# Splitting dt's weights ahead of the barrier, and projecting each last chunk behind the next chunk's moments

## The chip, the cores and the metric

One core of one Trainium2 chip runs the whole program in one launch. The metric is the device time in microseconds (us), median of the runs. All tensors are float32 in HBM; some are cut into three bfloat16 parts on the chip for TensorE.

## The reference, cut to what matters

Layer 0 is a linear attention over eight images of 128 x 128 x 128. Layer 1, the part that the change touches, is a selective scan:

```
xb  = silu(conv3x3(x @ Win[:, :256]) + conv_b)                     # the front
xs  = xb in 4 directions: rows, rows reversed, columns, columns reversed
dt, Bs, Cs = x_dbl[:8], x_dbl[8], x_dbl[9]      with x_dbl = xs @ Wxproj
delta = softplus(dt_weight @ dt + dt_bias)                         # the scan's first matmul
h_l = exp(delta * A) * h_(l-1) + delta * u * B_l ;   y_l = C_l * h_l + D * u
yz  = (sum of y over the directions) * silu(z)                     # "gate"
out = layernorm(yz) @ Wout                                         # "moments", then "project", "store"
```

The layer norm is over 256 channels, so it needs the mean of `yz` and of its square for each token before the result can be scaled; the product with `Wout` can be made before that and scaled afterwards.

## The kernel before, in words

The program has three stages: `layer0`, `layer1_front` and `layer1_scan`. In the last two, `in_order` fixes each engine's instructions, DMA issues included, in the order in which the Python code calls them. An engine or DMA queue that waits therefore holds up everything behind it. What decides about the time is the order inside `step` and which semaphore each instruction waits for.

**The front's end.** `layer1_front` walks eight images of 16 chunks. After an image, `leave(b)` writes its activation `ures` to HBM a second time with rows and columns exchanged: 32 copies into tiles named `turned` (line 635), done by ScalarE where `k % 5` is 1 or 3 and by VectorE otherwise, each followed by a 512 KB write on the SP queue (line 636). After copies 9 and 19, `split` cuts the rows of `dt`, `B` and `C` into three bfloat16 parts (lines 44, 46) and writes them (line 625). For the last image nothing else is left to be done, so the stage ends when the last `turned` write has landed.

**The scan's start.** A barrier over all engines (line 723) separates the stages. Behind it the SP queue loads the small tensors and `dt_weight` and `dt_bias` (line 737); VectorE splits both with `split3`, which is a cast, a subtraction, a cast, a subtraction and a cast; the six parts are written to HBM (lines 742, 744), and `weights` loads them back into the tiles `dtw` with ten small loads per direction (lines 825, 826). GpSimd clears these tiles first (line 760). Then SP issues `load_rows` (lines 865, 866) and `load` (line 872), which the first `delta` (line 883) and the first `weigh` (line 894) wait for.

**The scan's end.** N = 512 is the number of scan steps. When an image's last direction is done, its 16 chunks "leave" one per step: `leaving[n]` names the chunk of step n. For seven images that lies under the next image's scan. The last image's chunks leave in steps N to N+15 with nothing else to be done. I call these steps S0 to S15, and S16 the one after. In one of these steps the engines get, in this order:

- VectorE: `gate(now, 1)` (line 972: y times z, second half), `store` of the chunk before (line 1023, eight instructions into tile `r`), `variance(now)` (line 1005)
- ScalarE: `square(now, 1)` (line 975), `keep` (line 991, tile `sr`), `square_mean` (line 1001, `mv`), `square(next, 0)`
- TensorE: `moments(now)` (line 985, `pm`), `to_tokens(now)` (line 997, `pq`), `project(now)` (line 1017, `px`)
- GpSimd: `deviation` of the chunk before (lines 1009, 1010), `gate(next, 0)`, and in seven of the steps the DMA issue of `add_d` (line 856), which adds 1024 KB of `gs` to `y` in memory
- SP queue: two loads of `z` for the chunk after next (`fetch`, line 968), two stores to `out` (line 1027)

`pm` and `pq` share the one PSUM buffer with the tag `pt`, so the moments of a chunk also wait until `variance` of the chunk before has read `pq`. `z` has six buffers, two for each chunk, so `fetch` waits for the projection of the chunk three before it. `r` has two buffers, so a `store` waits until the store of the chunk before has landed.

Of the kernel before, what the change touches and what calls it, by code (L numbers as in the profile page):

```python
# [8 lines left out]
F32 = mybir.dt.float32  # L9
BF16 = mybir.dt.bfloat16  # L10
# [4 lines left out]
DRAM = bass.MemoryType.DRAM  # L15

P = 128
# [4 lines left out]
NC2 = 2  # L22
R = 8
K = 4
# [6 lines left out]
CH = 1024  # L31
# [9 lines left out]
def split3(nc, parts, x):  # L41

    for j in range(3):
        nc.vector.tensor_copy(parts[j], x)
        if j < 2:
            nc.vector.tensor_tensor(x, x, parts[j], ALU.subtract)
# [335 lines left out]


@with_exitstack
def layer1_front(ctx: ExitStack, tc, x1, win, conv_w, conv_b, wxp, d_par, ubs, xds, xps, gts, gs):

# [8 lines left out]
    nc = tc.nc  # L397
    const = ctx.enter_context(tc.tile_pool(name="l1c", bufs=1))
    big = ctx.enter_context(tc.tile_pool(name="l1b", bufs=1))
    wp = ctx.enter_context(tc.tile_pool(name="l1w", bufs=3))  # L400
# [34 lines left out]
    for j, d in enumerate(ON_PE):  # L435
        for c in range(NC2):
            dg = wp.tile([P, P], F32, name="dg1", tag="tb", bufs=4)
            nc.vector.tensor_scalar(dg, ident, cw[:, c, tap(*d) : tap(*d) + 1], None, ALU.mult)
            p = pm.tile([P, P], F32, name="pw", tag="m")
# [18 lines left out]
    N = B * NCH  # L458

    SEQ = (4, 6, 5, 7, 0, 1, 2, 3)  # L460
# [145 lines left out]
    def load_rows(b, i):  # L606
        r = slice(i * half, i * half + half)
        xws[b, i] = x = wp.tile([P, half, H], F32, name="xw", tag="d", bufs=2)
        nc.sync.dma_start(x, xds[b].rearrange("r (w h) -> w r h", h=H)[:, r, :])

    def split(b, i):

        r = slice(i * half, i * half + half)
        x = xws.pop((b, i))
        pt = pj.tile([P, half, P], F32, name="ptx", tag="pj")
        for j in range(half):
            nc.tensor.transpose(pt[:, j, :], x[:, j, :], ident)
        y = wp.tile([P, half, W], F32, name="xh", tag="tb", bufs=4)
        nc.scalar.copy(y, pt)
        for order, v in ((TURN, y), (NAT, x)):  # L620
            q = wp.tile([P, 3, half, P], BF16, name="parts", tag="tb", bufs=4)
            split3(nc, [q[:, j] for j in range(3)], v)
            dst = xps[b, order].rearrange("j r (a e) -> a j r e", e=P)
            for j in range(3):
                nc.sync.dma_start(dst[:, j, r, :], q[:, j])

    def leave(b):

        for i in range(2):
            load_rows(b, i)  # L630
        for k in range(NC2 * NCH):
            c, i = divmod(k, NCH)
            t = wp.tile([P, CW, W], F32, name="turned", tag="tc" if k % 3 == 2 else "tb", bufs=2 if k % 3 == 2 else 4)
            copy = nc.scalar.copy if k % 5 in (1, 3) else nc.vector.tensor_copy
            copy(t, uturn[:, c, i * CW : i * CW + CW, :])
            nc.sync.dma_start(ubs[b, TURN][c][:, i * CH : i * CH + CH], t.rearrange("p h w -> p (h w)"))
            if k % 10 == 9 and k < 20:
                split(b, k // 10)

    def step(n):  # L640

# [53 lines left out]


@with_exitstack
def layer1_scan(ctx: ExitStack, tc, ubs, xps, zs, gs, dtw, dtb, a_log, gamma, beta, w_out, out):

# [12 lines left out]
    nc = tc.nc  # L714
    const = ctx.enter_context(tc.tile_pool(name="l2c", bufs=1))
    big = ctx.enter_context(tc.tile_pool(name="l2b", bufs=1))
    wp = ctx.enter_context(tc.tile_pool(name="l2w", bufs=3))
    sm = ctx.enter_context(tc.tile_pool(name="l2s", bufs=4))
    px = ctx.enter_context(tc.tile_pool(name="l2px", bufs=3, space=PSUM))
    pe = ctx.enter_context(tc.tile_pool(name="l2pe", bufs=1, space=PSUM))  # L720
    dram = ctx.enter_context(tc.tile_pool(name="l2d", bufs=1, space=DRAM))

    tc.strict_bb_all_engine_barrier()

# [3 lines left out]
    nc.scalar.activation(sa, sa, AF.Exp)  # L728
    nc.vector.tensor_scalar(sa, sa, -1.0, None, ALU.mult)


    D2 = 2 * P
    wparts = dram.tile([3, R, K, D2], BF16, name="wparts")
    bparts = dram.tile([3, K, D2], BF16, name="bparts")
    for dst, src, rows in ((wparts, dtw.rearrange("k r d -> r k d"), R), (bparts, dtb.rearrange("o (k d) -> o k d", d=D2), 1)):
        x = wp.tile([rows, K, D2], F32, name="w32", tag="sp", bufs=2)
        nc.sync.dma_start(x, src)
        q = wp.tile([rows, 3, K, D2], BF16, name="w16", tag="ub", bufs=4)
        split3(nc, [q[:, j] for j in range(3)], x)
        for j in range(3):  # L740
            if rows == 1:
                nc.sync.dma_start(dst[j : j + 1], q[:, j])
            else:
                nc.sync.dma_start(dst[j], q[:, j])

# [10 lines left out]
    for i in range(3):  # L758
        t = const.tile([P, D2], BF16, name=f"dtw{i}")
        nc.gpsimd.memset(t, 0.0)  # L760
# [90 lines left out]
    ubt, sp, da = {}, {}, {}  # L851
# [122 lines left out]
    def square(m, hf):  # L974
        nc.scalar.activation(piece(m, hf), zt[m, hf], AF.Square)  # L975
# [56 lines left out]
    leaving, summed, fetched, weighed = {}, {}, {}, {}  # L1032
    for o in range(B):
        n = (o + 1) * K * NCH
# [11 lines left out]
    N = len(units)  # L1046

    def step(n):
        live = 0 <= n < N
        then = n + 1 < N  # L1050
        before = 1 <= n <= N
        now, last, soon, later = (leaving.get(n + i) for i in (0, -1, 1, 2))
        first = before and units[n - 1][0].place == 0
        if before:
            half1 = units[n - 1][0].first
            emit(n - 1, half1)
            if not first:
                gather(n - 1)
        if now and last:
            gate(*now, 1, nc.vector)  # L1060
        if before:
            emit(n - 1, 1 - half1)
        if n + 2 < N:
            load_rows(n + 2)
        if n in fetched:
            fetch(*fetched[n])
        if live:
            decay(n, 0)
        if now:
            square(now[1], 1)  # L1070
        if live:
            decay(n, 1)
            weigh(n, 0)
        if last:
            deviation(last[1])
        if live:
            weigh(n, 1)
        if now:
            moments(now[1])
        if live:  # L1080
            scan(n, 0)
            da.pop((n, 0))
        if last:
            for hf in range(2):
                store(*last, hf)
        if then:
            for c in range(NC2):
                delta(n + 1, c)
        if now:
            keep(now[1])  # L1090
        if then:
            soften(n + 1, 0)
        if now:
            to_tokens(now[1])
            square_mean(now[1])
        if then:
            soften(n + 1, 1)
        if live:
            scan(n, 1)
        if first:  # L1100
            ubt.pop(n - 1)
            if n + 3 < N:
                load(n + 3)
        if now:
            variance(now[1])
        if live:
            half1 = units[n][0].first
            spread(n, half1, "pc")
            spread(n, 1 - half1, "pt")
        if soon and now:  # L1110
            gate(*soon, 0, nc.gpsimd)
        elif soon:
            gate(*soon, 1, nc.gpsimd)
        elif later:
            gate(*later, 0, nc.gpsimd)
        if soon:
            square(soon[1], 0)
        if now:
            p = da.pop((n, 1)) if live else px.tile([P, CH], F32, name="px")
            for hf in range(2):  # L1120
                project(now[1], hf, p[:, hf * 512 : hf * 512 + 512])
        elif live and units[n][0].place == 0:
            da.pop((n, 1))
        if before and not first:
            add(n - 1)
            ubt.pop(n - 1)
        if n + 3 < N and not first:
            load(n + 3)
        if n in weighed:
            units[weighed[n]][0].weights()  # L1130
        if n in summed:
            add_d(*summed[n])
# [16 lines left out]
@with_exitstack  # L1149
def tile_kernel(ctx: ExitStack, tc, a, out):  # L1150
    dram = ctx.enter_context(tc.tile_pool(name="dram", bufs=1, space=DRAM))
    x1 = dram.tile([B, P, L], F32, name="x1")
    ubs = dram.tile([B, 2, NC2, P, L], F32, name="ubs")
    xds = dram.tile([B, R + 2, L], F32, name="xds")
    xps = dram.tile([B, 2, 3, R + 2, L], BF16, name="xps")
    zs = dram.tile([B, NC2, P, L], F32, name="zs")
    gts = dram.tile([2, NC2, P, NCH, NCH, CW * CW], F32, name="gts")
    gs = dram.tile([2, NC2, P, L], F32, name="gs")
    layer0(
        tc, a["x"], a["L0_conv_w_qkv"], a["L0_conv_w_out"], a["L0_conv_b_out"],  # L1160
        a["L0_conv_gamma"], a["L0_conv_beta"], a["L1_conv_Win"], x1, zs,
    )
    layer1_front(
        tc, x1, a["L1_conv_Win"], a["L1_conv_conv_w"], a["L1_conv_conv_b"], a["L1_conv_Wxproj"],
        a["L1_conv_D_param"], ubs, xds, xps, gts, gs,
    )
    layer1_scan(
        tc, ubs, xps, zs, gs, a["L1_conv_dt_weight"], a["L1_conv_dt_bias"], a["L1_conv_A_log"],
        a["L1_conv_gamma"], a["L1_conv_beta"], a["L1_conv_Wout"], out,
    )  # L1170

# [39 lines left out]
```

## Time and profile before

| what | value |
|---|---|
| median of 3 runs (lowest to highest) | 9557.71 us (9557.14 to 9560.87) |
| profiled execution: its own time / its span | 9559.43 us / 9557.7 us |
| busy: VectorE, GpSimd, ScalarE, TensorE | 85%, 75%, 75%, 66% |
| last `turned` write issued / first issue behind the barrier | 4835.1 us / 4840.8 us |
| first `rows` load of the scan issued | 4860.5 us |
| first and last `variance` of the last image (line 1005) | 9425.0 us / 9548.4 us |

Positions are microseconds from the start of the span. In timelines, a row is start, duration, engine, line, operation, output and inputs with shapes, and in brackets how long the engine had been idle and what ended that. Equal rows that follow closely are merged, with their count behind an x; such a row runs from the first start to the last end.

### The profile page before, as it was taken

How to read it: one execution, taken by the hardware profiler on the slowest of the kernel's cores; microseconds unless marked ns; L12 is line 12 of the kernel's file. 1: busy time of each engine (PE TensorE's matmuls, PEld its weight loads, DVE VectorE, ACT ScalarE, POOL GpSimd, SP SyncE). 2: the span in 40 equal slices, each digit the busy share in tenths (PEclk: the TensorE clock that was granted, in tenths of full speed). 3: DMA queues.
4: the chain of work that ended last, by engine and by line, in shares of the span. 5: the costliest groups of instructions: out<-in, count | busy, mean ns of one | idle time of the engine just before them, and what ended most of it. 6: DMA issues, size and time to landing. Idle time of an engine off the chain costs nothing. (4 is left out here: it accounts for less than half of the span.)

```text
span 9557.7 us, 89859 instructions
## 1 busy us (share of the span) xinstructions
PE 6331.1 (66%) x24352; PEld 3113.6 (33%) x24352; DVE 8131.2 (85%) x8188; ACT 7168.0 (75%) x8256; POOL 7193.5 (75%) x4361
## 2 busy tenths in 40 slices
PE   8999999988977788777923543636345363553736
PEld 5555655554322233222300321404123040220403
DVE  6667765563988898888979999999999999999996
ACT  5556655566977788777878888888888888888885
POOL 3445544454665488776849999999999999999997
PEclk9999999999988899888955665757557585665757
DMA  2332233313476678888765957759587695866858
GB/s 91 132 135 78 97 133 132 132 69 140 169 261 238 220 259 254 265 265 274 236 208 167 254 180 205 241 172 270 156 226 217 187 260 165 242 192 198 248 165 214
DMA packets 1034807, 1851.21 MB, mean 194 GB/s; under 512 B 274852, under 2 KB 500772, under 8 KB 1026112
## 3 DMA queue, kind: packets, MB, share of 16 engines
q1 hardware_dynamic: 999488, 1711.23, 54.1%
q0 software_dynamic: 34816, 134.23, 7.4%
q8 instruction: 199, 3.26, 0.1%
q14 instruction: 304, 2.49, 0.1%
HBM read 1153.03 MB, written 692.12 MB: 193 GB/s over the span
## 5 line engine op out<-in xcount | busy, mean ns | idle before, releaser
L894 POOL TENSOR_TENSOR ubt<-ubt,sp 128x1024 f32<-128x1024 f32 x1024 | 2458.0, 2458 | 157.9 <-ACT sp L887 90.7
L883 PE MATMUL px<-rows,dtw 128*128 128x512 bf16 x2048 | 952.9, 565 | 2234.3 <-DVE y L944 1062.6
L516 POOL TENSOR_TENSOR tap<-tap 128x1024 f32<-128x1024 f32 x512 | 1206.6, 2368 | 640.1 <-ACT tap L514 518.1
L524 DVE SCALAR_TENSOR_TENSOR acc<-xb,cw,acc 128x1024 f32<-128x1024 f32 x1024 | 1320.3, 1289 | 52.7 <-ACT tap L514 0.9
L887 ACT ACTIVATE sp<-px 128x1024 f32<-128x1024 f32 x1024 | 1046.0, 1024 | 419.0 <-PE px L883 344.3
L952 POOL TENSOR_TENSOR y<-y,ubt 128x512 f32<-128x512 f32 x768 | 1156.7, 1552 | 145.6 <-DVE ubt L925 145.3
L506 PE MATMUL acc<-xi,wt 128*128 128x512 f32 x2048 | 952.7, 608 | 385.8 <-ACT ures L531 385.4
L904 DVE TENSOR_TENSOR_SCAN ubt<-px,ubt 128x1024 f32<-128x1024 f32 x512 | 1176.5, 2330 | 25.4 <-POOL ubt L894 19.6
L902 DVE TENSOR_TENSOR_SCAN ubt<-px,ubt 128x1024 f32<-128x1024 f32 x512 | 1178.0, 2331 | 12.3 <-POOL ubt L894 6.1
L883 PEld LDWEIGHTS <-dtw 128*128 128x128 bf16 x2048 | 164.4, 109 | 3062.1 <-issue 868.4
L891 ACT ACTIVATE px<-sp,sa 128x1024 f32<-128x1024 f32 x1024 | 1110.2, 1109 | 6.1
L514 ACT ACTIVATE tap<-xb,cw 128x1024 f32<-128x1024 f32 x768 | 834.0, 1139 | 68.4 <-POOL tap L516 68.1
L887 ACT ACT_TABLE_LOAD x512 | 656.9, 1283 | 166.7 <-PE px L883 164.6
L282 POOL TENSOR_TENSOR q<-q,qs 128x512 f32<-128x512 f32 x256 | 272.0, 1063 | 638.5 <-DVE qs L281 638.5
L506 PEld LDWEIGHTS acc<-xi,wt 128*128 128x128 f32 x2048 | 383.8, 192 | 930.3 <-ACT ures L531 487.9
L891 ACT ACT_TABLE_LOAD x512 | 656.9, 1283 | 9.2
L1017 PEld LDWEIGHTS px<-wg,z 128*128 128x128 f32 x4096 | 560.5, 220 | 118.8 <-issue 113.7
L910 PE MATMUL pc<-rows,csel 128*128 128x512 bf16 x1024 | 515.5, 584 | 82.5 <-DVE rstd L1005 78.6
L1017 PE MATMUL px<-wg,z 128*128 128x128 f32 x4096 | 560.8, 303 | 0.0
L479 PE MATMUL pxb<-xi,wi 128*128 128x512 f32 x1024 | 495.8, 606 | 4.3 <-ACT xb L488 4.3
L944 DVE TENSOR_TENSOR y<-y,px 128x1024 f32<-128x1024 f32 x384 | 468.5, 1220 | 14.7 <-DVE px L932 0.5
L298 ACT ACTIVATE sq<-o 128x512 f32<-128x512 f32 x256 | 161.2, 630 | 423.0 <-DVE o L296 421.8
(155 smaller groups left out, 15151.2 us busy)
## 6 DMA issues: line engine op xcount, KB each, us to landing
ubt<-ubs SPq DMA_DIRECT2D x512, 1024.0 KB
zs<-z SPq DMA_DIRECT2D x512, 256.0 KB
ubs<-ures SPq DMA_DIRECT2D x256, 512.0 KB
ubs<-turned SPq DMA_DIRECT2D x256, 512.0 KB
z<-zs SPq DMA_DIRECT2D x256, 512.0 KB
y<-gs POOLq DMA_DIRECT2D x128, 1024.0 KB, 10.3
rows<-xps SPq DMA_DIRECT2D x1536, 60.0 KB
xi<-x SPq DMA_DIRECT2D x120, 576.0 KB
```

Of the source, the lines that this page charges most:

```text
L506: nc.tensor.matmul(acc[:, s, :], wt[:, j, c, :], x, start=(j == 0), stop=(j == len(ON_PE) - 1))
L514: nc.scalar.activation(t, at(n, c, *d), AF.Copy, scale=cw[:, c, tap(*d) : tap(*d) + 1])
L516: nc.gpsimd.tensor_tensor(sums[n, c], sums[n, c], t, ALU.add)
L524: nc.vector.scalar_tensor_tensor(acc, at(n, c, *d), cw[:, c, tap(*d) : tap(*d) + 1], acc, ALU.mult, ALU.add)
L883: nc.tensor.matmul(p[:, hf * 512 : hf * 512 + 512], sl.dw[:, c * P : c * P + P], src, start=True, stop=True)
L887: nc.scalar.activation(t, da[n, c], AF.Softplus)
L891: nc.scalar.activation(da[n, c], sp[n, c], AF.Exp, scale=sa[:, sl.s, c : c + 1])
L894: nc.gpsimd.tensor_tensor(ubt[n][:, c, :], ubt[n][:, c, :], sp.pop((n, c)), ALU.mult)
L902: nc.vector.tensor_tensor_scan(e[:, ::-1], x[:, ::-1], e[:, ::-1], start, ALU.mult, ALU.add)
L904: nc.vector.tensor_tensor_scan(e, x, e, start, ALU.mult, ALU.add)
L952: nc.gpsimd.tensor_tensor(v[:, c], v[:, c], h[:, c], ALU.add)
L1017: nc.tensor.matmul(po[:, w, :], z[:, c, w * H : w * H + H], wg[:, c, :], start=(c == 0), stop=(c == NC2 - 1))
```

## The change

The splitting of `dt_weight` and `dt_bias` moves from the scan's start into the last `leave` of the front, behind `turned` number 22. The instructions are the same, in other buffers. In the steps after N, `project` handles the chunk of the step before and stands behind `moments` and `keep` of the step's own chunk and ahead of `to_tokens`; `fetch` moves behind it. Step N has no projection any more, and step N+16 has one. For VectorE, ScalarE and GpSimd the order of the last steps stays as it was; on the SP queue too, fetch still stands ahead of store.

```
 layer1_front:
+    def split_weights():
+        D2 = NC2 * P
+        for dst, src, rows in (
+            (wparts, dtw.rearrange("k r d -> r k d"), R), (bparts, dtb.rearrange("o (k d) -> o k d", d=D2), 1),
+        ):
+            x = wp.tile([rows, K, D2], F32, name="w32", tag="ta", bufs=2)
+            nc.sync.dma_start(x, src)
+            qs = [
+                wp.tile([rows, K, D2], BF16, name=f"w16{j}", tag=tag, bufs=2)
+                for j, tag in enumerate(("d", "d", "ta"))
+            ]
+            split3(nc, qs, x)
+            for j in range(3):
+                nc.sync.dma_start(dst[j : j + 1] if rows == 1 else dst[j], qs[j])
...
     def leave(b):
...
             if k % 10 == 9 and k < 20:
                 split(b, k // 10)
+            if k == 22 and b == SEQ[-1]:
+                split_weights()
...
 layer1_scan:
-    for dst, src, rows in ((wparts, dtw.rearrange("k r d -> r k d"), R), (bparts, dtb.rearrange("o (k d) -> o k d", d=D2), 1)):
-        x = wp.tile([rows, K, D2], F32, name="w32", tag="sp", bufs=2)
-        nc.sync.dma_start(x, src)
-        q = wp.tile([rows, 3, K, D2], BF16, name="w16", tag="ub", bufs=4)
-        split3(nc, [q[:, j] for j in range(3)], x)
-        for j in range(3):
-            if rows == 1:
-                nc.sync.dma_start(dst[j : j + 1], q[:, j])
-            else:
-                nc.sync.dma_start(dst[j], q[:, j])
...
     def step(n):
...
-        if n in fetched:
+        if n in fetched and n <= N:
             fetch(*fetched[n])
...
             scan(n, 0)
             da.pop((n, 0))
+        if n > N:
+            if now:
+                keep(now[1])
+            p = px.tile([P, CH], F32, name="px")
+            for hf in range(2):
+                project(last[1], hf, p[:, hf * 512 : hf * 512 + 512])
+            if n in fetched:
+                fetch(*fetched[n])
         if last:
             for hf in range(2):
                 store(*last, hf)
...
-        if now:
+        if now and n <= N:
             keep(now[1])
...
-        if now:
-            p = da.pop((n, 1)) if live else px.tile([P, CH], F32, name="px")
+        if now and live:
+            p = da.pop((n, 1))
             for hf in range(2):
                 project(now[1], hf, p[:, hf * 512 : hf * 512 + 512])
```

More of the change, by code (lines that the diff above doesn't have):

```diff
@@ L384, in layer1_front @@
 @with_exitstack
-def layer1_front(ctx: ExitStack, tc, x1, win, conv_w, conv_b, wxp, d_par, ubs, xds, xps, gts, gs):
+def layer1_front(ctx: ExitStack, tc, x1, win, conv_w, conv_b, wxp, d_par, ubs, xds, xps, gts, gs, dtw, dtb, wparts,
+                 bparts):
     nc = tc.nc
@@ L697, in layer1_scan @@
 @with_exitstack
-def layer1_scan(ctx: ExitStack, tc, ubs, xps, zs, gs, dtw, dtb, a_log, gamma, beta, w_out, out):
+def layer1_scan(ctx: ExitStack, tc, ubs, xps, zs, gs, wparts, bparts, a_log, gamma, beta, w_out, out):
     nc = tc.nc
@@ L720, in layer1_scan @@
     pe = ctx.enter_context(tc.tile_pool(name="l2pe", bufs=1, space=PSUM))
-    dram = ctx.enter_context(tc.tile_pool(name="l2d", bufs=1, space=DRAM))
     tc.strict_bb_all_engine_barrier()
@@ L729, in layer1_scan @@
     nc.vector.tensor_scalar(sa, sa, -1.0, None, ALU.mult)
-    D2 = 2 * P
-    wparts = dram.tile([3, R, K, D2], BF16, name="wparts")
-    bparts = dram.tile([3, K, D2], BF16, name="bparts")
-    for dst, src, rows in ((wparts, dtw.rearrange("k r d -> r k d"), R), (bparts, dtb.rearrange("o (k d) -> o k d", d=D2), 1)):
-        x = wp.tile([rows, K, D2], F32, name="w32", tag="sp", bufs=2)
-        nc.sync.dma_start(x, src)
-        q = wp.tile([rows, 3, K, D2], BF16, name="w16", tag="ub", bufs=4)
-        split3(nc, [q[:, j] for j in range(3)], x)
-        for j in range(3):
-            if rows == 1:
-                nc.sync.dma_start(dst[j : j + 1], q[:, j])
-            else:
-                nc.sync.dma_start(dst[j], q[:, j])
+    D2 = NC2 * P
     NR = R + 2
@@ L1158, in tile_kernel @@
     gs = dram.tile([2, NC2, P, L], F32, name="gs")
+    wparts = dram.tile([3, R, K, NC2 * P], BF16, name="wparts")
+    bparts = dram.tile([3, K, NC2 * P], BF16, name="bparts")
     layer0(
@@ L1164, in tile_kernel @@
         tc, x1, a["L1_conv_Win"], a["L1_conv_conv_w"], a["L1_conv_conv_b"], a["L1_conv_Wxproj"],
-        a["L1_conv_D_param"], ubs, xds, xps, gts, gs,
+        a["L1_conv_D_param"], ubs, xds, xps, gts, gs, a["L1_conv_dt_weight"], a["L1_conv_dt_bias"],
+        wparts, bparts,
     )
     layer1_scan(
-        tc, ubs, xps, zs, gs, a["L1_conv_dt_weight"], a["L1_conv_dt_bias"], a["L1_conv_A_log"],
+        tc, ubs, xps, zs, gs, wparts, bparts, a["L1_conv_A_log"],
         a["L1_conv_gamma"], a["L1_conv_beta"], a["L1_conv_Wout"], out,
```

## The prediction

> **What bounds the kernel now.** The page's chain of waits gives VectorE 34% of the span, nearly all of it in the scan's body (lines 902, 904, 944), which the change leaves alone. So I read two short stretches: the stage boundary near 4840 us, and everything behind the last scan step at 9415 us.
>
> First the boundary, in the timeline:
>
> ```profile
> 4822.93 13.03 SPq L636 DMA_DIRECT2D ubs<-turned  x12
> 4840.82 0.39 SPq L727 DMA_DIRECT2D sa<-in_L_conv_A_log  x1
> ...
> 4843.74 1.50 DVE L44 CAST w<-w 8x1024 bf16<-8x1024 f32 x1 [1.94 <-DMA w<-in_L_conv_dt_weight]
> ...
> 4846.10 0.33 POOL L760 MEMSET dtw<- 128x256 bf16 x1
> ...
> 4849.20 1.38 SPq L825 DMA_DIRECT2D dtw<-wparts  x2
> ...
> 4854.45 2.29 SPq L825 DMA_DIRECT2D dtw<-wparts  x7
> ...
> 4857.16 2.97 SPq L825 DMA_DIRECT2D dtw<-wparts  x9
> 4860.17 0.27 SPq L826 DMA_DIRECT2D dtw<-bparts  x1
> 4860.48 1.21 SPq L865 DMA_DIRECT2D rows<-xps  x3
> ```
>
> The twelve last `turned` writes are bound by the DMA engines: from 4825 to 4839 us these are 101.6% busy at 404 GB/s, 1.25 us for each write. Behind the barrier they lie idle, and the SP queue is the path: it waits for VectorE's split, part by part, and issues the rows only at 4860.48 us.
>
> Then the last chunks. First the timeline of an undisturbed step, S1:
>
> ```profile
> 9431.03 1.05 PE L997 MATMUL pq<-sel,sr 128*128 128x4 f32 x8 [0.76 <-ACT sr L991]
> ...
> 9431.95 3.82 PE L1017 MATMUL px<-wg,z 128*128 128x128 f32 x32
> 9432.12 0.18 ACT L1001 ACTIVATE mv<-pq 128x8 f32<-128x8 f32 x1 [1.14 <-PE pq L997]
> ...
> 9432.33 0.17 DVE L1005 TENSOR_TENSOR rstd<-pq,mv 128x8 f32<-128x8 f32 x1 [1.65 <-ACT mv L1001]
> 9432.42 1.21 DVE L972 TENSOR_TENSOR z<-y,z 128x1024 f32<-128x1024 f32 x1
> ...
> 9433.67 1.06 ACT L975 ACTIVATE y<-z 128x1024 f32<-128x1024 f32 x1 [0.41 <-DVE z L972]
> ```
>
> Then S7, which began with TensorE idle: VectorE's timeline, and the chain of waits behind it.
>
> ```profile
> 9478.22 0.15 DVE L1005 TENSOR_TENSOR rstd<-pq,mv 128x8 f32<-128x8 f32 x1
> 9478.30 1.21 DVE L972 TENSOR_TENSOR z<-y,z 128x1024 f32<-128x1024 f32 x1
> ```
>
> ```profile
> 9479.57 3.00 PE pm L985 x14
> 9482.65 0.59 ACT sr L991
> ```
>
> In S1 TensorE never waits for VectorE. While it projects (3.69 us in the chain), variance, the next chunk's gate and its square run beside it, done at 9434.73. A step is moments 1.90 + copy to `sr` with its gaps 0.68 + `pq` 1.05 + projection 3.69 = 7.35 us. But line 1005 runs from 9425.0 to 9548.4, which is 15 steps of 8.23: up to S11 the DMA engines are the bound. While an `add_d` runs they serve little else:
>
> ```profile
> q0 software_dynamic: 228, 0.93, 96.6%
> q1 hardware_dynamic: 198, 0.11, 9.6%
> ```
>
> (9433.5 to 9438.5 us: packets, MB, share.) Stores to `out` wait behind it, `store` waits 31.6 us in all for a free `r`, and the groups of three steps that begin with the moments at 9428.4, 9452.7 and 9478.5 take 24.3, 25.8 and 26.1 us.
>
> **What the Trainium skill says.** "DMA: Bandwidth & Descriptors", section "Queues, rings and completion order": each DMA engine takes turns between the queue rows that have work. The trace agrees that neither queue is shut out, but a turn is not an equal share of bytes: 0.93 MB against 0.11. The same page, "Issuing engines are not separate DMA queues": transfers from all issuers share 16 engines, so moving an issue creates no bandwidth; shares near 100% from two queues together agree. "SBUF — State Buffer", section "SBUF: two separate sides": VectorE casts and GpSimd exclude each other on a shared port. The trace fits: the cast above takes 1.50 us beside GpSimd's memsets, the last one of the same shape, with GpSimd idle, 0.67.
>
> **The change part by part.** All three sums are against the profiled execution, 9559.43 us (span 9557.7), 1.72 above the median.
>
> *1. Splitting inside the last `leave`: +14.4 us.* No work is added, but the SP queue now holds, between `turned` writes 22 and 23: a load, three stores that wait for VectorE, a load, three more. Nine writes of 512 KB are queued behind them, and the barrier waits for those. Write 22 is issued at 4823.9 with the earlier writes' data still in the engines until about 4827.5; the load behind it lands near 4828.7 (about 1.2 us after its data). A split is 3 casts x 0.67 + 2 subtractions x 1.21 + gaps 0.2 = 4.65 us: done 4833.4. The third store goes out at 4833.6, the bias load at 4833.9; it lands 2.0 us after its issue's end (4841.75 to 4843.74 above), 4836.2. Second split: 4840.85. Write 23 is issued near 4841.25 instead of 4824.7 and its data start near 4842.5. ScalarE's copies 23, 26 and 28 are done by then; VectorE's at 1.03 us keep ahead of the engines' 1.25. So nine writes end at 4842.5 + 9 x 1.25 = 4853.75 instead of 4839.4. Cover: only the 3 to 4 us of data in flight. Bounds: +12 (a quicker load) to +17 (slow landings of the six small stores, none of which the trace shows under load).
>
> *2. The scan's start without the split: -7.5 us.* The SP queue has issued the other small loads by 4842.8 and then waits for GpSimd's memset of `dtw`, done at 4846.43. Twenty loads at 0.335 (2.97 for nine, with gaps) take 6.7: rows at 4853.0 instead of 4860.48. Everything behind follows the rows and the `ubt` loads on the same queue. VectorE's constants are off the path. Bounds: -8 (memsets quicker without the casts) to -6 (a load waits for an earlier one's landing).
>
> *3. The projection behind the next moments: +24.8 us.* TensorE saves the wait for `sr`: 1.90 + 3.69 + 1.05 = 6.64 of work instead of 7.35. But the projection was the cover for variance, gate and square. VectorE keeps its order: `gate(n+1, 1)` stands behind `variance(n)`, which needs `pq(n)`, now behind `project(n-1)`. The loop closes: `variance(n)` to the end of the next moments 4.39 us (S7 above, 9478.22 to 9479.57 + 3.00 + a gap of 0.04: gate, square, then the rest of the moments 2.0), projection 3.69, start of `pq` to start of variance 1.30 (9431.03 to 9432.33) = 9.38 us a step. `store` ends about 1.1 us after the projection, beside `pq`. `deviation` is ready 3 us into the step, `gate(next, 0)` on GpSimd at 5.4; neither counts. 15 steps: 140.7, against 123.4 now: +17.3.
>
> Then the transfers. Three steps need about 26 us of DMA engine time (now they fill 26.1) and get 28.1, so the bound moves to the loop, but not wholly: `add_d` starts about 7 us into a step and holds the engines 6 us, the two `z` loads (issued after each half of the projection, so about 2 us later in the step than now) and then the stores stand behind it. A walk from variance 9425.2: the `add_d` of S1 holds the engines from 9432.5 to 9439, the `z` loads of S1 end at 9441, its stores land at 9443 and 9444. S2 wants to store again at 9440.7 and 9442.5, waits, and ends its stores at 9445, so variance (and the gate queued behind it) comes at 9445.1 instead of 9443.9: 1.2 us late. The second `add_d` of the pair delays S3 in the same way by 0.9. With three pairs and one single: 3 x 2.1 + 1.2 = 7.5. Bounds: 0 to 19 in all, above by the 13.2 us that one such wait costs now. S16 ends like S15 now, since `pq(15)` is followed at once by the projection in both.
>
> Sum: 14.4 - 7.5 + 24.8 = +31.7; 9559.43 + 31.7 = 9591.1 for a like execution, 9589.4 against the median. I say 9590.
>
> **The rivals.**
>
> *The sequencing pays (not slower; 8%).* If the gate and square of chunk n+1 were ready before `pq(n)` ends, TensorE would run 6.64 us a step. With the DMA engines as the bound up to S11, that gives 4 or 5 steps x 0.71 = 3.5 us, at most 15 x 0.71 = 10.6. With the boundary's +6.9, the result is +3.4 to -3.7: no change. It decides if a step's variance-to-moments stretch falls under 6.64 - 3.69 - 1.30 = 1.65 us instead of 4.39. For it speaks that TensorE does wait 0.7 us for `sr` in each step now; against it VectorE's fixed order.
>
> *The split is hidden (5%).* If the engines had 15 us of writes queued, part 1 would cost nothing: -7.5 + 24.8 = +17.3. Against: six buffers of `turned` hold at most 7.5 us.
>
> *Transfers and clock (12%).* The out stores find the engines taken in every step, and TensorE, idle 2.7 us of each step, loses clock: in the dry S10 the granted clock was 0.81 and the moments took 4.95 us. Stalls at the upper bound of 19 instead of 7.5, or a projection of 4.5 us in all steps (15 x 0.85 = 12.7): +43 to +45.
>
> **How the numbers follow.** The loop with moderate stalls has 75%: 9573 to 9606 from part 1 (12 to 17), part 2 (-8 to -6) and part 3 (17 to 36), not all at one end. Adding the third rival's values up to 9610 and leaving out the first gives 9573 to 9610. The measurement of this kernel can tell about 0.2%, 19 us, from no change. Slower by more: the loop but for its lowest edge, and the third rival, 0.85. Within: the first rival and most of the second, 0.13. Faster by more than 0.2% needs the first rival's best and a free split together, 0.02.
>
> **What would show it.** Right: in the timeline after, about 17 us from `turned` write 22 to write 23, most of it with the DMA engines idle; the first rows load about 12.3 us behind the barrier's first issue instead of 19.7; line 1005 at 9 to 10 us a step, the moments' last wait ended by ScalarE's square or VectorE's gate, and "`r` waits for out" well under 31.6 us. Wrong: line 1005 at 7 to 8 us a step (the loop isn't closed), a gap on the SP queue under 10 us (part 1), or steps over 11 us (the transfers still bind).

## The result, and the profile after

| | before | after |
|---|---|---|
| median of 5 runs each (lowest to highest) | 9558.67 us (9557.14 to 9561.59) | 9601.57 us (9594.09 to 9617.73) |
| ratio, with its 95% interval | | 1.0044 (1.0033 to 1.0056) |
| profiled execution: time / span | 9559.43 / 9557.7 us | 9608.05 / 9606.2 us |
| first issue behind the barrier | 4840.8 us | 4853.9 us |
| first `rows` load of the scan | 4860.5 us | 4865.9 us |
| first to last `variance` of the last image | 123.4 us | 163.0 us |

The changed kernel is 42.9 us slower by the medians, where +32 was forecast. The totals of one kernel scatter: code that is the same reached `turned` write 20 anywhere between 4821.2 and 4833.9 us in the profiled executions below. So small effects are read as stretches between two fixed points of one trace, not from totals. There is one trace of each kernel; where two kernels share the code of a stretch, its length agreed within about 2 us at the end and 1.2 us at the boundary. One of the 13 runs of `front_early` took 13222 us in a slower state of the chip and is left out of its ratio. In `step` and its helpers, line numbers of after are 5 higher than those of before: `variance` is 1010, `store` 1028, moments 990, the projection 1022, the gate 977.

The boundary after the change, in the timeline:

```profile
4823.13 1.66 SPq L653 DMA_DIRECT2D ubs<-turned  x3
4824.84 1.13 SPq L635 DMA_DIRECT2D w<-in_L_conv_dt_weight  x1
...
4829.68 4.19 SPq L642 DMA_DIRECT2D wparts<-w  x3
...
4835.99 4.14 SPq L642 DMA_DIRECT2D bparts<-w  x3
4840.24 9.17 SPq L653 DMA_DIRECT2D ubs<-turned  x9
4853.92 0.38 SPq L745 DMA_DIRECT2D sa<-in_L_conv_A_log  x1
```

and behind the barrier, in the timeline of SP:

```profile
4865.94 1.21 SPq L870 DMA_DIRECT2D rows<-xps  x3
```

The queue holds write 23 back from 4824.8 to 4840.2 us. What the DMA engines do meanwhile is in the table of windows (columns: window, its length, busy us with counts for TensorE, its weight loads, VectorE, ScalarE and GpSimd, granted clock, DMA share, GB/s):

```profile
4828.00:4840.20 12.20, 0.00 (x0) 0.00 (x0) 9.25 (x11) 1.96 (x1) 0.00 (x0) 0.50 0.03 6
```

A DMA share of 0.03: for 12 us next to nothing flows, and nothing covers VectorE's split (part of its 9.25 us). Afterwards the barrier comes 13.1 us later than before, and the rows follow it in 12.02 us instead of 19.66. Net +5.46.

Now the end. VectorE's timeline in S3 and S4:

```profile
9466.15 2.16 DVE L1028 SCALAR_TENSOR_TENSOR r<-px,rstd,bw 128x128 f32<-128x128 f32 x8 [6.91 <-PE px L1022]
9468.22 0.16 DVE L1010 TENSOR_TENSOR rstd<-pq,mv 128x8 f32<-128x8 f32 x1
...
9476.42 2.16 DVE L1028 SCALAR_TENSOR_TENSOR r<-px,rstd,bw 128x128 f32<-128x128 f32 x8 [6.91 <-PE px L1022]
9478.49 0.16 DVE L1010 TENSOR_TENSOR rstd<-pq,mv 128x8 f32<-128x8 f32 x1
```

From `variance` to `variance` is 10.27 us. The bracket says what sets it: VectorE stood idle 6.91 us for the projection, then ran all eight instructions of `store`, and only then the variance behind them, with no idle time between. The chain of waits of the same step closes the loop:

```profile
9468.52 1.02 PE pm L990 x2
...
9469.56 2.99 PE pm L990 x14
9472.56 3.78 PE px L1022 x32
...
9476.42 0.15 DVE r L1028
```

Moments, projection, `store`, variance, moments. `pq` and its wait, which the forecast had as the last link, are not on it. Over the whole end (9450 to 9607 us), the waits (us in total, times, longest) say the same, and that `out` is no longer the first concern:

```profile
DVE r L1028 <- PE px L1022: 89.9, 13, 8.3
DVE r L1028 <- DMA out<-r: 16.4, 2, 8.3
```

Seven of the fifteen steps are 10.27 us, within 0.01; the other eight add 8.9 us. The windows of S4, S6 and S7:

```profile
9468.20:9478.50 10.30, 8.57 (x56) 5.28 (x56) 3.39 (x12) 2.77 (x4) 6.34 (x4) 1.00 0.60 143
9488.80:9500.40 11.60, 8.57 (x56) 5.27 (x56) 3.31 (x11) 2.77 (x4) 5.13 (x3) 1.00 1.00 254
9500.40:9512.00 11.60, 9.88 (x56) 5.77 (x56) 3.38 (x11) 2.77 (x4) 6.35 (x4) 0.85 0.56 123
```

S6 has the full clock and a DMA share of 1.00. It is 1.4 us longer because `store` waits for `out`:

```profile
9498.34 2.16 DVE L1028 SCALAR_TENSOR_TENSOR r<-px,rstd,bw 128x128 f32<-128x128 f32 x8 [8.29 <-DMA out<-r]
```

S7 has half-free DMA engines, but the clock is 0.85 and the same 56 matmuls are busy 9.88 us instead of 8.57. S9 is of the first kind; S1, S2, S8, S11 and S12 are of the second (clock 0.76 to 0.85).

### The profile page after: what moved, and what is told of

Same layout as the page of the kernel before. It is cut to its first block, busy times and chain, and to the rows that moved or that the text cites. A ratio compares the mean times of both kernels' runs of the same rounds, so it can differ in the third digit from the quotient of the medians.

```text
span 9606.2 us, 89691 instructions
## 1 busy us (share of the span) xinstructions
PE 6325.4 (66%) x24190; PEld 3124.4 (33%) x24352; DVE 8130.0 (85%) x8188; ACT 7167.5 (75%) x8256; POOL 7193.4 (75%) x4361
## 5 line engine op out<-in xcount | busy, mean ns | idle before, releaser
L888 PE MATMUL px<-rows,dtw 128*128 128x512 bf16 x1893 | 911.1, 574 | 2267.0 <-DVE y L949 1069.0
L949 DVE TENSOR_TENSOR y<-y,px 128x1024 f32<-128x1024 f32 x384 | 468.7, 1220 | 14.4
```

The source lines that it names most:

```text
L888: nc.tensor.matmul(p[:, hf * 512 : hf * 512 + 512], sl.dw[:, c * P : c * P + P], src, start=True, stop=True)
L949: nc.vector.tensor_tensor(v, v, ts.pop(n), ALU.add)
```

## The experiments

Each group of kernels was measured beside runs of before of its own. Their medians are 9567.71 us for the first four kernels, 9566.33 for the next four and 9568.28 for the last two, against 9558.67 beside the changed kernel. So ratios are compared below, not times from different groups.

**One part alone.** `front_only` is the changed kernel with `step` as before; `tail_only` is the kernel before with only the changes in `step`. The code below shows only the start of what differs.

```
 front_only, against after:
-        if n > N:
-            ...
-                project(last[1], hf, ...)
+        if now:
+            p = da.pop((n, 1)) if live else px.tile([P, CH], F32, name="px")
 tail_only, against after:
-    def split_weights():
-    ...
+    for dst, src, rows in ((wparts, ...), (bparts, ...)):    # in layer1_scan
```

> The split of dt's weights moved into the last image's turned writes as in the changed kernel, the last chunks in the order of before. Theory (the two sites add up, each as the trace of after shows it): first issue behind the barrier 12.9 us later, first rows load +5.5 us, end +5 to +7 us, with the runs as close together as those of before (some 5 us). Rival (part of the loss at the end comes from the shifted start, through another phase of the transfers in the scan's body): +10 us or more, and the steps of the last image no longer 8.2 us on average.

> The split as before, the last chunks in the order of the changed kernel. Theory: a step closes a loop of 10.27 us (variance to the end of the next moments 4.4, projection 3.8, store 2.1), plus some us for transfers and for a lower clock of TensorE: 15 steps take 155 to 165 us instead of 123.4, the end comes 33 to 43 us later, and the runs scatter over 10 us or more. Rival (the scatter and part of the loss belong to the split at the boundary): under +30 us, runs within 5 us.

Measured: `front_only` 9574.01 us, ratio 1.0007 (0.9999 to 1.0015); from `turned` write 20 to the first rows 42.98 us (before 37.55, after 42.81); first to last variance 123.9. `tail_only` 9610.69 us, ratio 1.0044 (1.0031 to 1.0056); 37.55 at the boundary, 162.7 at the end. So the two parts are not seen to act on each other: each stretch has its value of before or of after, according to which part is in. The front's part costs 5.4 us net, the end some 39. What was expected of the scatter did not come: the runs of `front_only` lie 28 us apart, those of before beside them 26.

**Is it `store` that closes the loop?** In `tail_only` both halves of a projection lie in one PSUM tile `px`. `tail_pair` gives each half its own. `tail_late` moves `store` of chunk n-2 to the step's start, behind the gate, out of the way of the variance.

```
 tail_pair, against tail_only:
-            p = px.tile([P, CH], F32, name="px")
             for hf in range(2):
-                project(last[1], hf, p[:, hf * 512 : hf * 512 + 512])
+                p = px.tile([P, CH], F32, name="px")
+                project(last[1], hf, p[:, 0:512])
 tail_late, against tail_only:
             gate(*now, 1, nc.vector)
+        if n > N + 1:
+            for hf in range(2):
+                store(*leaving[n - 2], hf)
...
-        if n > N:
+        if last and n > N:
...
-        if last:
+        if last and n <= N:
             for hf in range(2):
                 store(*last, hf)
...
-        for n in range(N + NCH + 1):
+        for n in range(N + NCH + 2):
```

> As tail_only, with each half of a chunk's projection in a PSUM tile of its own. Theory A (the store waits for the whole projection only because both halves lie in one tile): the first four store instructions run under the second half, the store ends 1.1 us behind the projection, variance comes 1.3 us behind it, and a step takes 9.4 us instead of 10.27: 12 to 14 us less than tail_only. Theory B (the store waits for the last matmul however the halves lie): no difference from tail_only beyond 4 us.

> As tail_only, with every store one step later: on VectorE it stands behind the next but one chunk's gate instead of ahead of variance. Theory (it is the store, 2.1 us behind the projection, that delays variance, and gate and moments with it): a step takes 9.4 us instead of 10.27, 12 to 14 us less than tail_only in 15 steps, less some us for the extra store at the end. Rival (variance waits for pq behind the projection in any case, or transfers fill what is saved): within 4 us of tail_only.

Measured: `tail_pair` 9597.70 us, ratio 1.0033 (1.0021 to 1.0046), 154.5 from first to last variance, an undisturbed step 9.18. `tail_late` 9589.28 us, ratio 1.0022 (1.0013 to 1.0030), 141.0 from first to last, a step 9.16. VectorE's timeline of `tail_pair`:

```profile
9558.55 1.13 DVE L1023 SCALAR_TENSOR_TENSOR r<-px,rstd,bw 128x128 f32<-128x128 f32 x4 [5.12 <-PE px L1017]
9560.28 1.13 DVE L1023 SCALAR_TENSOR_TENSOR r<-px,rstd,bw 128x128 f32<-128x128 f32 x4 [0.60 <-PE px L1017]
9561.33 0.16 DVE L1005 TENSOR_TENSOR rstd<-pq,mv 128x8 f32<-128x8 f32 x1
...
9570.51 0.16 DVE L1005 TENSOR_TENSOR rstd<-pq,mv 128x8 f32<-128x8 f32 x1
```

The x8 has become two groups of x4, and the first begins in the middle of the projection. That is the picture that the forecast had taken for the changed kernel itself; it needs two tiles. With one tile, all eight wait for its last matmul. In `tail_late` the same line waits for something else:

```profile
9487.89 0.17 DVE L1005 TENSOR_TENSOR rstd<-pq,mv 128x8 f32<-128x8 f32 x1 [5.78 <-ACT mv L1001]
...
9497.05 0.17 DVE L1005 TENSOR_TENSOR rstd<-pq,mv 128x8 f32<-128x8 f32 x1 [5.40 <-ACT mv L1001]
```

Now ScalarE's `mv`, made from `pq`, releases the variance, as the forecast's loop has it. So `store` between the projection and the variance is what a step pays, about 1.1 us. The two kernels differ in what is left over. In the stretch of `tail_pair` only 8 of the 16.4 us come out (the medians give 13.0, where 12 to 14 were expected, but its runs lie 17 us apart). 15 steps of 9.18 would take 137.7 us, and 16.8 are added. About 6 of these are longer busy time of TensorE at clocks of 0.74 to 0.84; the rest goes with the transfers (`store` waits 45.7 us in all for `out`, and steps reach 12.6 and 13.0). `tail_late`, which stores a step later, gains more than expected, 21.7 us in the stretch. Of these, 16.7 are the shorter loop; it also had a low clock in one step only, and only 3.6 us are added to its 15 steps of 9.16.

**Is it the clock in the other steps?** `tail_warm` adds six matmuls of 512 columns behind `to_tokens`, where TensorE would wait for the variance; their product is not used.

```
 tail_warm, against tail_only:
             to_tokens(now[1])
+            if n >= N:
+                w = pe.tile([P, GN], F32, name="warm", tag="pc")
+                for _ in range(6):
+                    nc.tensor.matmul(w, csel, rws[0][:, 0:512], start=True, stop=True)
```

> As tail_only, with six extra 128x512 bfloat16 matmuls into an unused PSUM bank behind each step's pq; nothing reads their result. Theory (in the changed order TensorE idles 2.7 us or more of each step, loses clock in about six of fifteen steps, and this costs 6 to 7 us of the last stretch): the granted clock stays at 1.0 from the third step on, every step without a wait for a store takes 10.3 us, and variance 0 to 15 takes 155 to 159 us instead of 162.7. Rival (the long steps come from transfers, the low clock is a by-effect): the same steps stay at 10.7 to 11.7 us and the stretch at 161 us or more.

Measured: 9601.25 us, ratio 1.0037 (1.0024 to 1.0050); 159.85 from first to last variance, 2.8 us less than `tail_only`. That lies between the 155 to 159 expected and the 161 or more of the rival. Only S1 (0.80) and S7 (0.85) still have a low clock, instead of six steps of `tail_only`; a plain step is 10.27 as in that kernel. The steps with a low clock took 5.3 us more than plain ones in `tail_only` and take 2.1 here; those in which `store` waits for `out` took 3.3 and take 3.6. So the clock accounts for a few us of the end, not for its bulk.

**Does the split have to lie bare?** `front_early` loads weights and bias as nine rows of one tile at the start of the last `leave`, splits them once behind copy 12 (five VectorE instructions instead of ten), and issues the six stores behind write 22. As in after, the scan's own split is gone.

```
 front_early, against before:
+    def load_weights():
+        dts.append(wp.tile([R + 1, K, D2], F32, name="w9", tag="ta", bufs=2))
+        nc.sync.dma_start(dts[0][0:R], dtw.rearrange("k r d -> r k d"))
+        nc.sync.dma_start(dts[0][R : R + 1], dtb.rearrange("o (k d) -> o k d", d=D2))
...
     def leave(b):
+        if b == SEQ[-1]:
+            load_weights()
...
+            if k == 12 and b == SEQ[-1]:
+                split_weights()
+            if k == 22 and b == SEQ[-1]:
+                store_weights()
```

> The last chunks as before. The weights and the bias are loaded together at the start of the last image's turned writes, split together behind the 13th copy (five VectorE instructions instead of ten), and their six stores stand behind turned write 22, where their data are ready. Theory (the cost at the boundary is the SP queue's wait for loads and splits, not the work): from turned write 20 to the first rows load 29 to 31 us instead of 37.5, against 42.9 with the changed kernel's split. Rival (extra small stores between the big ones, or VectorE's extra 4.7 us, hold the writes up as well): 34 us or more.

Measured: 9566.21 us, ratio 0.9997 (0.9989 to 1.0005). In SP's timeline the wait ahead of write 23 is gone:

```profile
4826.40 1.66 SPq L661 DMA_DIRECT2D ubs<-turned  x3
...
4831.66 9.14 SPq L661 DMA_DIRECT2D ubs<-turned  x9
...
4857.49 1.21 SPq L880 DMA_DIRECT2D rows<-xps  x3
```

From write 20 to the rows: 31.09 us, where before has 37.55 and after 42.81. The split lies ahead of write 20 here; measured from VectorE's first `turned` copy, it is 73.28 against 78.75, a gain of 5.5, and after has 82.98, a loss of 4.2. These are not exact to better than a microsecond or so: of the seven kernels with the boundary of before, three need 36.4 us from write 20 to the rows instead of 37.55. So moving the work is worth some 5 us when nothing on SP's queue waits for it, and costs about as much when the queue does. How much of the gain comes from the halved number of instructions was not separated. In the total the gain cannot be told from nothing.

**Can the end be made to pay?** `tail_open` is meant to take the gate and square of the next chunk out of the loop: for n > N the whole gate and square of chunk n+1 stand behind the projection and ahead of `variance`, `pq` has a PSUM buffer other than that of the moments, and `store` is last.

```
 tail_open, against before:
+        if n > N:
+            if now:
+                keep(now[1])
+            ...                                   # project(last), fetch, as in after
+            if soon:
+                gate(*soon, 1, nc.vector)
+                gate(*soon, 0, nc.gpsimd)
+                square(soon[1], 0)
+                square(soon[1], 1)
+            if now:
+                to_tokens(now[1], "pc")
+                square_mean(now[1])
+                variance(now[1])
         if last:
             for hf in range(2):
                 store(*last, hf)
```

`tail_open_z` also frees `fetch` of its wait for a projection: in the last steps `z` is loaded into a third kind of tile, four whole chunks deep, at the step's start. `both_open` and `both_open_z` are these two with the front of `front_early`.

```
 tail_open_z, against tail_open:
+            both = wp.tile([P, NC2, CH], F32, name="zend", tag="ub", bufs=4)
...
-        if n in fetched and n <= N:
-            fetch(*fetched[n])
+        if n in fetched:
+            fetch(*fetched[n], n > N)
```

> The split as before. In the steps after N the projection stands behind the next moments as in the changed kernel, but the next chunk's second gate and both squares stand ahead of pq and variance, variance stands ahead of the store, and pq has a PSUM bank of its own, so that no loop runs from variance through gate to moments. Theory: TensorE's own work sets an undisturbed step, 6.6 to 6.8 us instead of 7.35; up to the eleventh step the DMA engines bind at about 26 us for three; variance 0 to 15 takes 117 to 123 us against 123.4, the end 2 to 6 us earlier than before. Rival (the later z loads of this order starve the gates, so that transfers bind in every step): 125 us or more.

> The boundary of front_early and the last chunks of tail_open. Theory: both gains add, 7 us at the boundary and 2 to 6 at the end: 9 to 13 us under the kernel before. Rival (the earlier start of the scan is lost again in the transfers of its body): within 4 us of the kernel before.

> As tail_open, with the last image's later z tiles in the four buffers that the scan's ubt no longer needs, so that fetch stands at the start of its step and waits for no projection. Theory (in tail_open the gates starve because a z load waits for a projection that the new order made later): waits for z fall from 51 us in all to under 15, undisturbed steps take 6.6 to 7.0 us, and variance 0 to 15 takes 117 to 126 us instead of 137. Rival (the loads are late because the engines are taken by add_d and the stores, whenever they are issued): waits for z stay above 30 us and the stretch above 130.

> The boundary of front_early and the last chunks of tail_open_z. Theory: turned write 20 to first rows load 31 us instead of 37.5, last scan to end 138 to 146 us against 144.7 with the kernel before; in all 5 to 12 us under the kernel before, if the rest of the kernel scatters no more than its own runs. Rival: within 4 us of it or slower.

| kernel | median, us | ratio (95%) | first to last variance, us |
|---|---|---|---|
| `tail_open` | 9581.67 | 1.0015 (1.0008 to 1.0021) | 137.0 |
| `both_open` | 9578.11 | 1.0012 (1.0005 to 1.0018) | 136.5 |
| `tail_open_z` | 9565.27 | 0.9995 (0.9987 to 1.0004) | 124.9 |
| `both_open_z` | 9563.71 | 0.9991 (0.9983 to 0.9999) | 122.9 |

Three of the four expectations failed. `tail_open` was to be 2 to 6 us faster than before and `both_open` 9 to 13; they are 15 and 12 slower. `both_open_z` was to gain 5 to 12 us and gained 4.6 by the medians, with an interval of 1 to 16. `tail_open_z` came into its range for the stretch, but not for the waits.

In `tail_open` some steps take 6.66 to 7.04 us, near the forecast's sum of TensorE's work (6.64). Yet the stretch is 13.6 us longer than in before. Its waits:

```profile
DVE z L972 <- DMA z<-zs: 34.4, 9, 7.3
POOL z L972 <- DMA z<-zs: 16.4, 3, 7.9
```

50.8 us of waiting for `z`: `fetch` waits for a projection, that projection now comes a chunk later, and the gate needs the data earlier. With the loads freed of that, in `tail_open_z`:

```profile
POOL zend L978 <- DMA zend<-zs: 12.9, 3, 7.4
DVE zend L978 <- DMA zend<-zs: 11.4, 7, 5.1
```

Half of the waiting is left, 24.3 us where under 15 were expected, although a load is issued two chunks ahead as in before and waits for no projection. The stretch takes 124.9 us, where before has 123.4. S2 to S12 take 92.3 us, against 94.0, and the DMA share is 0.90 or more in each of them but S7 (0.75). That agrees with the DMA engines as the bound of these steps. Loads issued further ahead were not tried.

But where the engines are free, the order is not open either. S14 has a DMA share of 0.24 and the full clock, and takes 7.75 us, where an undisturbed step of before takes 7.35. The timeline shows why:

```profile
9545.88 0.25 POOL L1015 TENSOR_SCALAR rstd<-rstd 128x8 f32<-128x8 f32 x1 [2.39 <-DVE rstd L1011]
9546.21 1.66 POOL L1016 TENSOR_TENSOR rstd<-rstd,half 128x8 f32<-128x8 f32 x1
...
9547.81 1.21 DVE L978 TENSOR_TENSOR zend<-y,zend 128x1024 f32<-128x1024 f32 x1
9547.84 3.40 POOL L978 TENSOR_TENSOR zend<-y,zend 128x1024 f32<-128x1024 f32 x1
...
9551.27 2.00 ACT L981 ACTIVATE y<-zend 128x1024 f32<-128x1024 f32 x2 [3.11 <-POOL zend L978]
...
9553.37 0.17 DVE L1011 TENSOR_TENSOR rstd<-pq,mv 128x8 f32<-128x8 f32 x1 [4.35 <-ACT mv L1007]
```

Another loop has closed: variance, `deviation` on GpSimd, GpSimd's gate, both squares on ScalarE, `mv` behind them, variance. GpSimd's gate takes 3.40 us here, where it starts with VectorE's gate; six steps with 3.34 to 3.40 us take 7.71 to 7.88. In the four steps of 6.85 to 7.05 us it takes 2.35, and VectorE's gate starts later. So the shorter steps are those in which data came late for one gate, and the 6.64 us of TensorE's work was not had with both gates in time; only S15, which has no next chunk to gate, takes 6.66. What an order without this loop would gain was not measured.

## Why the prediction was right or wrong

The direction, the likeliest case and the range were right; the time was 11.6 us short by the medians. Against the profiled executions, as the forecast made its sum, +31.7 stands against +48.6 us, of which 0.2 lie ahead of write 20:

| step | forecast | measured | from |
|---|---|---|---|
| 1, splitting in the last `leave` | +14.4 | +12.9 | barrier, from `turned` write 20 |
| 2, the scan's start without it | -7.5 | -7.6 | barrier to rows, 12.02 against 19.66 |
| the scan's body | 0 | +4.6 | rows to first variance |
| 3, first to last variance | +24.8 | +39.6 | 163.0 against 123.4 |
| behind the last variance | 0 | -1.1 | 8.17 against 9.31 |

- **Steps 1 and 2 held**, within their bounds. Most of the front's 1.5 us come from a second split that ended at 4839.9 instead of 4840.85, and write 23 going out at 4840.24 instead of 4841.25. The small stores were issued as their parts were ready. One reading was loose: 512 KB at 404 GB/s take 1.30 us, not 1.25; over nine writes that is 0.4 us.
- **The body** is the same code in both. From the rows to the first variance it takes 4564.5 us in before, 4569.1 in after, and from 4558.0 (`tail_open`) to 4572.4 (`front_early`) in the others: scatter, which no forecast of this change could hold.
- **Step 3 had the right mechanism and a mis-sized loop.** The sentence that failed is "`store` ends about 1.1 us after the projection, beside `pq`". All eight instructions start after the projection's last matmul, and the variance, behind them on VectorE, starts 2.15 us after it. A step is 10.27 us instead of 9.38. `tail_late` and `tail_pair` put the rest of the loop at 9.16 and 9.18, so the other links were 0.2 us too dear and `store` costs 1.1 us a step. (The forecast's four terms of a step of before add up to 7.32 us, not 7.35; the trace has 7.35, and nothing hangs on it.)
- **The transfers were over-sized**: 2.6 us in S6 and S9 instead of 7.5. The slower loop leaves the DMA engines more room (share 0.68 over the end, 0.88 in before). `tail_pair`, with the loop that the forecast had meant, lost 16.8 us (154.5 - 15 x 9.18), some 6 of it to the clock. So for its own loop the walk was some 3 us too small.
- **The clock**, which the forecast left to the third rival, took 6.4 us in six steps; TensorE's busy time is longer by the same 6.4 us in them.

The sum closes: 24.8, less 3.3 for the other links (15 x 0.22), plus 16.6 for `store` (15 x 1.11), less 4.9 for the transfers, plus 6.4 for the clock is 39.6. In part it was luck that the time was not further off: the loop and the transfers were wrong in opposite directions.

Of the forecast's signs, the wait on the SP queue (16.2 us from write 22 to write 23), the rows 12.0 us behind the barrier and the shorter wait for `out` came. A step of 9 to 10 us did not. One sign of being wrong came too: six steps are over 11 us, two of them by transfers and four by the clock.

Of the rivals, "The sequencing pays" fell in the changed kernel: from the variance to the end of the next moments takes 4.3 us, not under 1.65. Whether it would pay in an order without any such loop stays open: `tail_open_z`, with a loop through GpSimd, gained nothing that can be told from scatter. "The split is hidden" fell: a DMA share of 0.03. "Transfers and clock" named the total of the medians (+43 to +45) with the wrong causes: neither were the stores to `out` waiting in every step nor did the projection take 4.5 us; it takes 3.84 at either clock.

## What to carry to other kernels

When a step is moved behind another, write down which instruction of each in-order engine now waits for it, and count in full what stands between that instruction and the next link of the loop: here eight instructions that had been free became 1.1 us in each of fifteen steps. Ask what the readers of a tile wait for: where a tile holds two halves, a reader of the first half may wait for the second. An order that opens one loop can close another: after a change, read the chain of an undisturbed step again. And work that waits can stand in an idle stretch for nothing only if its issuing queue need not wait for it: load early, compute early, and issue the store when the data are long there.

## What was not expected of the hardware

The granted clock fell to 0.84 or 0.85 for pairs of steps (S1 and S2 with 0.76 and 0.85, S7 and S8, S11 and S12), and only the moments felt it: from the first of them to the projection's start 3.96 us in S6, 5.27 in S7, 4.61 in S8, while the projection took 3.84 in all three. What starts such a pair is not settled: TensorE had been idle for 3.07 us ahead of S7's moments, but for only 1.68 ahead of S11's, as ahead of S3's to S5's with the full clock, and the 2.86 us ahead of S10's were followed by the full clock too. Extra matmuls made such steps rarer (two instead of six) and did not remove them.

In `tail_open_z` the gates on VectorE and GpSimd held each other up. Where both started within 0.1 us of each other, VectorE's took 1.21 us and GpSimd's 3.34 to 3.40. Where GpSimd's started first by 0.4 to 1.8 us, it took 2.35 us and VectorE's 1.68 to 3.04. It looks like what the prediction reads in a VectorE cast beside GpSimd's memsets, but no run here was made to test it.
